# Five output buffers in layer 1's expert blocks, and layer 2's front with transposes a group ahead and additions on GpSimd

## The chip, the core and the metric

The kernel runs on one core of one Trainium2 chip, with its engines TensorE (PE in the profile; PEld is its weight load), VectorE (DVE), ScalarE (ACT), GpSimd (POOL) and SyncE (SP, here only a queue for transfers). The metric is the device time of one execution in microseconds: 1908.99 us before the change, the median of three runs (1906.96 to 1911.32). Beside these runs stands one profiled execution, from which all durations and positions come. Positions are microseconds from the start of its span.

## The reference, cut to what matters

Four layers work on x of 2708 rows and 256 columns, each with a graph part over a 2708 x 2708 adjacency matrix and then a feed-forward part:

```python
x = x + L1_gnn(layernorm(x), adj)
x = x + L1_ffn(layernorm(x))       # H = gelu(x W1); each row goes to one of 8 experts: prob * (H Wd[e] + bd[e])
x = x + L2_gnn(layernorm(x), adj)  # h = x W^T; masked attention from a_src, a_dst; elu(w @ h)
x = x + L2_ffn(layernorm(x))
```

The change lies at the end of L1_ffn and at the start of L2_gnn. For the latter, every row of h and two scores (the row's products with attn_src and attn_dst) must be there. All arithmetic is float32.

## The kernel before

x stays in SBUF as 22 tiles of 128 rows (the last has 20). A scheduling layer fixes at build time in which order each engine's instructions stand; that order need not be the order of the code, and each engine then works strictly in its own order. Tiles come from pools: a tile name has `bufs` places, and a new tile must wait until the readers of the one that had its place are done.

**Layer 1's expert blocks** (`Units`, lines 630 to 724). Rows are sorted by expert into blocks of 128. For each block GpSimd fetches 128 row names and weights (L519), then the 128 rows of H (tile `hs`, 512 KB, L659). SyncE loads the expert's weights and bias (`wb`, 1152 KB, three places, L1063); the load is left out where the place already holds that expert. TensorE turns `hs` (L670) and ScalarE copies the result to `hTs` (L671); TensorE then multiplies by `wb` into `yacc` (L719, two places). VectorE adds the bias and scales by the probability, into `ys` (L716, L720, L721), which has two places, and GpSimd scatters `ys` into the DRAM tensor `given` (L505). So block n + 2 can write its `ys` only once the scatter of block n has landed. `wb` comes free when L720 has read the bias from it. In the profile 24 blocks run; a conditional rest (L626) is not entered.

**Layer 2's front** (L1415 to L1446) goes over six groups of tiles, called g0 to g5 below: tiles 0 and 1, then four tiles each (`FOURS`). For a group it

- loads its rows of `given` into `mine` (two places, L56 and L61) on SyncE's queue, the first behind all scatters;
- adds them to x on VectorE, two tiles at a time (L1425);
- turns each tile on TensorE (L213), and ScalarE copies it to `xT4` (L214), one copy of 256 columns a tile;
- takes mean and variance (`stats`, L186, L187) and ScalarE makes 1/sqrt (L141, `var`);
- multiplies by the weights, 258 columns wide (`times`, L260), each tile into a PSUM bank of its own, `ps_acc`, of which there are five (`psum_pool(sums, 3, 5)`); transposes use three other banks, `ps_tmp`;
- scales the two score columns on ScalarE (`sc`, L1437, two places, cleared by GpSimd, L1433), turns them (L1354), copies them to one small tile (L1356) and sends them to DRAM (`row_scores`, L1357);
- reads them back broadcast to all partitions (`Rb`, L1361) and takes exp (`row_factor`, L1367);
- makes exps of the column scores (`hh`'s last column, `G`, `rowe`), and VectorE writes the scaled rows of `hh` out of `ps_acc` (L1445). Only then is that bank free.

**Layer 2's attention loop** (L1498 on) follows: VectorE makes `e` from `Rb`, `G` and the mask (L1506), and TensorE multiplies it with `hh` into five `ps_acc` banks at once (L1514).

Of the kernel before, what the change touches and what calls it, by code (L numbers as in the profile page):

```python
# [8 lines left out]
F32 = mybir.dt.float32  # L9
# [3 lines left out]
ALU = mybir.AluOpType  # L13
AX = mybir.AxisListType

P = 128
N = 2708
D = 256
DC = D // P
E = 8  # L20
NT = (N + P - 1) // P
W = 512
# [14 lines left out]
def rows(t):  # L37
    return min(P, N - t * P)
# [8 lines left out]
FOURS = [range(0, 2)] + [range(t, min(t + 4, NT)) for t in range(2, NT, 4)]  # L47
# [19 lines left out]
def adj_ffn4(ctx: ExitStack, tc: tile.TileContext, a: dict, out: bass.AP):  # L67
    nc = tc.nc
    v, s, g, te = nc.vector, nc.scalar, nc.gpsimd, nc.tensor

    const = ctx.enter_context(tc.tile_pool(name="const", reuse_waits="tile", bufs=1))
    work = ctx.enter_context(tc.tile_pool(name="work", reuse_waits="tile", bufs=3))
# [9 lines left out]
    def ps_tmp():  # L82
        if "spare" in pools:

            pools["spare"] += 1
            if pools["spare"] % 3 == 1:
                return pools["psum"].tile([P, 2, W], F32, name="num", bufs=2)[:, 0, :]
            if pools["spare"] % 3 == 2:
                return pools["psum"].tile([P, W], F32, name="den", bufs=2)
        return pools["psum"].tile([P, W], F32, tag="tmp", name="ps_tmp", bufs=pools["tmp"])  # L90
# [4 lines left out]
    ident = const.tile([P, P], F32, name="ident")  # L95
# [17 lines left out]
    x = const.tile([P, NT, D], F32, name="x")  # L113
# [26 lines left out]
    def lnexp(out, in_, func, **kw):  # L140
        i = s.activation(out, in_, func, **kw)  # L141
        tc.add_manual_dep(i.ins, pinned[-1].ins.name, mybir.DependencyInfo(
            mybir.DependencyClass.NoSync, mybir.DependencyReason.DATA), reason="table")
# [33 lines left out]
    def stats(tiles, src=None, by_log=False):  # L177


        G = len(tiles)  # L180
        mv = small.tile([P, G, 2], F32, name="mv", tag=f"mv{G}", bufs=2)
        v.memset(mv[:, G - 1, :], 1.0)
        for i, t in enumerate(tiles):
            r = rows(t)
            st = small.tile([P, 6], F32, name="st")
            v.bn_stats(st[:r], x[:r, t, :] if src is None else src[:r, i, :])  # L186
            v.bn_aggr(mv[:r, i, :], st[:r])  # L187
        var = small.tile([P, G], F32, name="var", tag=f"var{G}", bufs=2)
        if by_log:
            lnexp(var, mv[:, :, 1], AF.Ln, bias=eps)  # L190
            lnexp(var, var, AF.Exp, scale=-0.5)
            return mv, var
        v.tensor_scalar(var, mv[:, :, 1], EPS, None, op0=ALU.add)
        return mv, rsqrt(small, var, G)
# [14 lines left out]
    def turn_to(xT, xn, r, bank=None):  # L209

        p = ps_tmp() if bank is None else bank
        for c in range(DC):
            te.transpose(p[:, c * P : c * P + r], xn[:, c * P : (c + 1) * P], ident[:r, :r])  # L213
        s.copy(xT, p[:, : DC * P].rearrange("p (c t) -> p c t", c=DC)[:, :, :r])  # L214
# [297 lines left out]
    def behind(i, past):  # L512
        for p in past:
            tc.add_manual_dep(i.ins, p.name, mybir.DependencyInfo(
                mybir.DependencyClass.Sync, mybir.DependencyReason.DATA), reason="scattered rows")
# [114 lines left out]
    class Units(Blocks):  # L630
# [3 lines left out]
        def __init__(self, pool, given, weights, hidden):  # L634
            Blocks.__init__(self, pool, given, weights)
            self.hidden, self.named, self.places, self.got = hidden, [], [0, 0], None

            self.names = pool.tile([P, MOST, 2], F32, name="names")
            g.memset(self.names, 1.0)
            self.hs = [pool.tile([P, HC * P], F32, name="hs", tag="hs", bufs=3) for _ in range(3)]  # L640
            for h in self.hs:
                g.memset(h, 0.0)
            self.ik, self.ok = "taken1", "given1"

        def fetch_names(self, item):
            (_, ix, *_), b, past, src, full = item
# [54 lines left out]
        def pieces(self, pool, during=None):  # L701

            turned = [self.turn(pool, self.rows[0][1])]
            yield
            n = 0
            while self.rows:
                if len(self.rows) > 1:
                    turned.append(self.turn(pool, self.rows[1][1]))
                    yield
                w2, hT = self.ahead.pop(0), turned.pop(0)  # L710
                m, _ = self.rows.pop(0)
                self.more()
                if during is not None:
                    during(n)
                n += 1
                y = pool.tile([P, D], F32, name="ys", bufs=2)  # L716
                q = pools["psum"].tile([P, W], F32, name="yacc", bufs=2)[:, :D]
                for f in range(HC):
                    te.matmul(q, lhsT=hT[:, f, :], rhs=w2[:, f, :], start=(f == 0), stop=(f == HC - 1))  # L719
                v.tensor_tensor(y, q, w2[:, HC, :], ALU.add)  # L720
                i = v.tensor_scalar(y, y, m[:, 1:2], None, op0=ALU.mult)  # L721
                self.last = i.ins.name
                scatter(self.given, m[:, 0:1].bitcast(I32), y, self.given.shape[0] - 1, self.ok)
                yield
# [20 lines left out]
    for size, full in ((2 * P, True), (2 * P, False), (P, True), (P, False)):  # L745
        steps[size, full] = const.tile([P, NT], F32, name=f"steps{size}{full}")
        v.tensor_scalar(steps[size, full], count[:, :NT], float(size), float(size - 1) if full else 0.0,
                        op0=ALU.mult, op1=ALU.add)
# [36 lines left out]
    with ExitStack() as l0:  # L785
# [19 lines left out]
        gp = gnn.enter_context(tc.tile_pool(name="g0", reuse_waits="tile", bufs=3))  # L805
# [83 lines left out]
        for tiles in GROUPS:  # L889
            end = tiles is GROUPS[-1]  # L890
            own = [(t, (t - tiles[0]) * P, P) for t in tiles if t < FULL]
# [6 lines left out]
            for j in range(FULL):  # L898
                r = rows(j)
                ad = gp.tile([P, GMAX * P], F32, name="adrow", bufs=5)[:r, :w]  # L900
                i = nc.sync.dma_start(ad, a["adjT"][j * P : j * P + r, c0 : c0 + w])
# [19 lines left out]
                y = gp.tile([P, GMAX * P], F32, name="y", bufs=3)[:r, :w]  # L921
                wt = gp.tile([P, GMAX * P], F32, name="wt", bufs=4)[:r, :w]
                weigh(ad, y, wt, r)
                for p, pair in zip(acc, pairs):
                    for n in pair:
                        if n == len(own):
                            continue
                        _, k, q = own[n]
# [21 lines left out]
            for p, pair in zip(acc, pairs):  # L950
                if pair[0] == len(own):
                    continue
                t, m, q = own[pair[0]][0], len(pair), own[pair[-1]][2]
# [68 lines left out]
        for q, t0, t1 in ((P, 0, FULL), (LAST, FULL, NT)):  # L1022
            d = ps_tmp()
            for t in range(t0, t1):
                i = te.matmul(d[:q, t : t + 1], lhsT=cs[:, t * P : t * P + q], rhs=ones,
                              start=(t == t0), stop=(t == t1 - 1))
# [17 lines left out]
    with ExitStack() as l1:  # L1044
# [25 lines left out]
        gp = gnn.enter_context(tc.tile_pool(name="g1", reuse_waits="tile", bufs=2))  # L1070
# [279 lines left out]
    def row_scores(kept, scores, t0, n):  # L1350


        p = ps_tmp()
        te.transpose(p[:n, :P], scores, ident)  # L1354
        er = w_l1[:n, 0, :P]
        s.copy(er, p[:n, :P])  # L1356
        nc.sync.dma_start(kept.rearrange("t h c -> (t h) c")[t0 : t0 + n, :], er)  # L1357
# [6 lines left out]
    def row_factor(dst, kept, h, t0, n):  # L1364

        row_read(dst, kept, h, t0, n)
        lnexp(dst, dst, AF.Exp, scale=0.8)  # L1367
# [6 lines left out]
    with tc.tile_pool(name="t3", reuse_waits="tile", bufs=1) as t3:  # L1374
# [34 lines left out]
        with tc.tile_pool(name="g2", reuse_waits="tile", bufs=1) as gp:  # L1409
# [2 lines left out]
            rowe = gp.tile([P, NT, 1], F32, name="rowe")  # L1412
            Rb = gp.tile([P, NT * P], F32, name="Rb")
            kept = tc.dram_tile([NT, 1, P], F32, name="rows2")
            for tiles in FOURS:  # L1415
                n, t0 = len(tiles), tiles[0]
                o = gp.tile([P, 4, D], F32, name="mine", bufs=2)
                for i in load_tiles(nc, o, tiles, given[1], t0):
                    behind(i, scattered["given1"])
                for k in range(0, n, 2):  # L1420
                    for q, m in (((P, 2),) if rows(t0 + k + 1) == P else
                                 ((P, 1), (rows(t0 + k + 1), 1))):
                        i = k if q == P else k + 1
                        xs = x[:q, t0 + i : t0 + i + m, :]
                        v.tensor_tensor(xs, xs, o[:q, i : i + m, :], ALU.add)  # L1425
                xT = gp.tile([P, DC, W], F32, name="xT4", bufs=2)
                own = tiles_of(t0 * P, (n - 1) * P + rows(tiles[-1]))
                for t, k, r in own:
                    turn_to(xT[:, :, k : k + r], x[:r, t, :], r)
                rstd = stats(tiles, by_log=True)[1]  # L1430

                sc = gp.tile([P, 4, 2], F32, name="sc", bufs=2)
                g.memset(sc, 0.0)  # L1433
                ps = []
                for i, (t, k, r) in enumerate(own):
                    ps.append(times(xT, k, r, w_l2, D + 2, ps_acc()))
                    s.activation(sc[:r, i, :], ps[-1][:, D:], AF.Copy, scale=rstd[:r, i : i + 1])  # L1437
                row_scores(kept, sc[:, :n, 1], t0, n)
                row_factor(Rb[:, t0 * P : (t0 + n) * P], kept, 0, t0, n)
                lnexp(hh[:, t0 : t0 + n, D], sc[:, :n, 0], AF.Exp)  # L1440
                lnexp(G[:, t0 : t0 + n, 0], sc[:, :n, 0], AF.Exp, scale=-0.8)

                lnexp(rowe[:, t0 : t0 + n, 0], sc[:, :n, 1], AF.Exp, scale=-0.2, bias=ln8)
                for i, (p, (t, k, r)) in enumerate(zip(ps, own)):
                    v.tensor_scalar(hh[:r, t, :D], p[:, :D], rstd[:r, i : i + 1], hh[:r, t, D :],  # L1445
                                    op0=ALU.mult, op1=ALU.mult)  # L1446

            spread_out(hh[:, FULL, :])
            spread_out(G[:, FULL, :])
# [593 lines left out]
```

## Time and profile before

| what | value |
|---|---|
| runs | 1908.99 us, median of 3 |
| profiled execution | 1918.45 us; its span 1916.7 us |
| granted TensorE clock | 0.983 |
| busy: PE, PEld, DVE, ACT, POOL | 1826.6, 1326.0, 1097.8, 642.8, 344.1 us |
| layer 1's expert blocks: first to last product | 964.8 to 1084.5 us |
| last scatter issued; first load of `mine` issued | 1085.6; 1091.5 us |
| layer 2's front: first transpose to last product | 1095.1 to 1128.9 us |
| layer 2's attention loop begins | 1128.8 us |

The profiled execution took 9.5 us more than the median. "Busy" of TensorE includes the pipelined end of each matmul, so that a stage can be almost all busy and still have room. In the trace one fp32 product of a tile with a 128-row half of the weights is two matmul records, and a transpose is one; a tile's product with all 256 rows is thus four records.

### The profile page before, as it was taken

How to read it: one execution, taken by the hardware profiler on the slowest of the kernel's cores; microseconds unless marked ns; L12 is line 12 of the kernel's file. 1: busy time of each engine (PE TensorE's matmuls, PEld its weight loads, DVE VectorE, ACT ScalarE, POOL GpSimd, SP SyncE). 2: the span in 40 equal slices, each digit the busy share in tenths (PEclk: the TensorE clock that was granted, in tenths of full speed). 3: DMA queues.
4: the chain of work that ended last, by engine and by line, in shares of the span. 5: the costliest groups of instructions: out<-in, count | busy, mean ns of one | idle time of the engine just before them, and what ended most of it. 6: DMA issues, size and time to landing. Idle time of an engine off the chain costs nothing.

```text
span 1916.7 us, 25790 instructions
## 1 busy us (share of the span) xinstructions
PE 1826.6 (95%) x9453; PEld 1326.0 (69%) x9453; DVE 1097.8 (57%) x2498; ACT 642.8 (34%) x1459; POOL 344.1 (18%) x406
## 2 busy tenths in 40 slices
PE   7999998999999999999979799999899999999998
PEld 6888777888888888888778578888566632232344
DVE  6777862443433625354532265555355398999897
ACT  7868751222222303113222232222232551031131
POOL 1004254333322001303356300000000000000000
PEclk9999999999998999999989899999899999999999
DMA  8435656887773554544758410000101000000000
GB/s 276 139 109 161 219 187 223 318 331 279 279 284 107 178 150 121 142 105 136 211 161 319 141 50 1 1 1 1 44 1 34 17 1 23 23 12 28 20 20 16
DMA packets 88846, 233.33 MB, mean 122 GB/s; under 512 B 18015, under 2 KB 44679, under 8 KB 80648
## 3 DMA queue, kind: packets, MB, share of 16 engines
q1 hardware_dynamic: 71752, 189.18, 29.9%
q0 software_dynamic: 16960, 42.42, 7.0%
q8 instruction: 78, 1.28, 0.3%
q14 instruction: 56, 0.46, 0.1%
HBM read 216.29 MB, written 28.71 MB: 128 GB/s over the span
## 4 chain that ended last, share of the span: by engine, by line
PE 42%; DVE 2%; DMA 2%; ACT 2%; issue 1%; another core or an unknown queue 1%; POOL 0%; SPq 0%; POOLq 0%; DVEq 0%; ACTq 0%
PE num L1941 10%; PE ps_acc L1514 9%; PE den L1951 6%; PE ps_tmp L367 4%; PE ps_acc L1704 3%; PE yacc L719 3%; PE ps_tmp L260 2%; DMA L_ffn_beta<-in_L_ffn_beta 1%; PE ps_acc L670 1%; PE ps_acc L260 1%; PE ps_tmp L213 1%; DVE e L1911 1%; DVE e L1506 0%; ACT wh L1843 0%
## 5 line engine op out<-in xcount | busy, mean ns | idle before, releaser
L1911 DVE SCALAR_TENSOR_TENSOR e<-arena,G,mask 128x1024 f32<-128x1024 f32 (+1 forms) x264 | 287.0, 1149 | 13.6 <-PE den L1951 13.6
L1941 PE MATMUL num<-e,wh 128*64 128x512 f32 (+4 forms) x1056 | 215.8, 551 | 0.0
L1514 PE MATMUL ps_acc<-hh,e 128*128 128x257 f32 x882 | 199.2, 382 | 1.7 <-ACT o L1457 1.7
L1300 PE MATMUL acc<-sup,adrow 128*128 128x256 f32 x882 | 200.1, 384 | 0.4 <-DVE adrow L1268 0.4
L929 PE MATMUL acc<-msg,wt 128*128 128x256 f32 x882 | 198.6, 381 | 2.0 <-DVE wt L887 1.2
L1300 PEld LDWEIGHTS acc<-sup,adrow 128*128 128x128 f32 x882 | 166.0, 191 | 29.1 <-issue 5.6
L929 PEld LDWEIGHTS acc<-msg,wt 128*128 128x128 f32 x882 | 165.2, 190 | 28.4 <-issue 2.1
L1514 PEld LDWEIGHTS ps_acc<-hh,e 128*128 128x128 f32 x882 | 163.6, 190 | 29.2 <-ACT o L1457 4.3
L617 PE MATMUL yacc<-wb,hTs 128*128 128x256 f32 x736 | 170.6, 383 | 6.2 <-issue 3.4
L583 PE MATMUL ps_acc<-xTs,wa 128*128 128x256 f32 (+1 forms) x768 | 169.3, 373 | 5.8 <-DVE xTs L573 3.1
L585 ACT ACTIVATE hTs<-ps_acc,wa 128x256 f32<-128x256 f32 (+1 forms) x192 | 88.8, 465 | 247.1 <-PE yacc L617 164.5
L583 PEld LDWEIGHTS ps_acc<-xTs,wa 128*128 128x128 f32 x768 | 136.5, 190 | 32.1 <-DVE xTs L573 5.6
L617 PEld LDWEIGHTS yacc<-wb,hTs 128*128 128x128 f32 x736 | 138.3, 192 | 25.3 <-issue 3.8
L1941 PEld LDWEIGHTS num<-e,wh 128*64 128x64 f32 (+1 forms) x1056 | 66.5, 136 | 127.3 <-issue 105.6
L1506 DVE SCALAR_TENSOR_TENSOR e<-Rb,G,mask 128x640 f32<-128x640 f32 (+2 forms) x110 | 85.1, 774 | 90.5 <-PE ps_acc L1514 90.4
L1951 PE MATMUL den<-e,wh 128*32 128x512 f32 (+4 forms) x1056 | 118.0, 548 | 0.0
L214 ACT COPY xT<-ps_tmp 128x256 f32<-128x256 f32 x98 | 33.6, 365 | 235.9 <-PE ps_tmp L213 218.3
L1265 DVE TENSOR_SCALAR mask<-adrow 128x1024 uint8<-128x1024 f32 (+1 forms) x66 | 41.4, 627 | 123.2 <-DMA adrow<-in_adjT 122.8
L719 PE MATMUL yacc<-wb,hTs 128*128 128x256 f32 x384 | 88.7, 385 | 1.1 <-DMA wb<-in_L_ffn_Wdp 1.1
L887 DVE SCALAR_TENSOR_TENSOR wt<-adrow,wt 128x640 f32<-128x640 f32 (+3 forms) x67 | 71.1, 1063 | 27.5 <-ACT wt L141 19.8
L1951 PEld LDWEIGHTS den<-e,wh 128*32 128x32 f32 (+1 forms) x1056 | 30.2, 108 | 77.9 <-issue 73.8
L619 DVE TENSOR_TENSOR ys<-yacc,wb 128x256 f32<-128x256 f32 x46 | 19.5, 424 | 112.7 <-PE yacc L617 103.4
(457 smaller groups left out, 2618.7 us busy)
## 6 DMA issues: line engine op xcount, KB each, us to landing
adhalf<-in_adjT SPq DMA_DIRECT2D x42, 677.0 KB
wb<-in_L_ffn_W2p SPq DMA_DIRECT2D x24, 1152.0 KB
wb<-in_L_ffn_Wdp SPq DMA_DIRECT2D x24, 1152.0 KB
wa<-in_L_ffn_W1b SPq DMA_DIRECT2D x24, 1028.0 KB
adrow<-in_adjT SPq DMA_DIRECT2D x42, 512.0 KB
adrow<-in_adjT SPq DMA_DIRECT2D x42, 320.0 KB
adrow<-in_adjT SPq DMA_DIRECT2D x21, 576.0 KB
adrow<-in_adjT SPq DMA_DIRECT2D x21, 448.0 KB
```

What stands on the lines that cost most here:

```text
L367: te.matmul(p[:, :w], lhsT=w1[:, c, f * P : (f + 1) * P], rhs=xnT[:, c, c0 : c0 + w], start=(c == 0), stop=(c == DC - 1))
L583: i = te.matmul(p[:, f % 2, : m * P], lhsT=w1[:, c, f * P : (f + 1) * P], rhs=xT[:, c, : m * P], start=(c == 0), stop=(c == DC - 1))
L585: s.activation(hT[:, f, : m * P], p[:, f % 2, : m * P], AF.Gelu, bias=bias[:, f : f + 1])
L617: te.matmul(q[:, k, :], lhsT=hT[:, f, k * P : (k + 1) * P], rhs=w2[:, f, :], start=(f == 0), stop=(f == HC - 1))
L719: te.matmul(q, lhsT=hT[:, f, :], rhs=w2[:, f, :], start=(f == 0), stop=(f == HC - 1))
L929: te.matmul(p[:q, n - pair[0], :], lhsT=wt[:, k : k + q], rhs=msg[:r, j, :], start=(j == 0 and n == pair[0]), stop=(j == FULL - 1 and n == ...
L1300: te.matmul(p[:q, n - pair[0], :], lhsT=ad[:, k : k + q], rhs=sup[:, jj, :], start=(jj == 0 and n == pair[0]), stop=(jj == FULL - 1 and n ...
L1506: i = v.scalar_tensor_tensor(e[:r, :w], Rb[:r, c0 : c0 + w], G[:r, j, :], mask[:r, j, c0 : c0 + w], op0=ALU.max, op1=ALU.mult)
L1514: te.matmul(p[:, : D + 1], lhsT=e[:, k : k + q], rhs=hh[:, j, :], start=(j == 0), stop=False)
L1911: v.scalar_tensor_tensor(e[:, :w], slow[:, m % 2, k, :w], G[:, j, 2 * pair + k, :], mask[:, j, c0 : c0 + w], op0=ALU.max, op1=ALU.mult)
L1941: te.matmul(num[k * DK : (k + 1) * DK, hf, :q], lhsT=wh[some, j, 2 * pair + k, :DK], rhs=e[some, h0 - c0 : h0 - c0 + q], start=(j == 0), s ...
L1951: te.matmul(den[z : z + Q, :q], lhsT=wh[some, i, 2 * pair + k, DK : DK + 1] .to_broadcast([some.stop - some.start, Q]), rhs=e[some, h0 - c ...
```

## The change

Layer 1: the block counter `outputs` gives three of every five blocks a `y` from another pool, the tile `xn` of `work`, which has three places; two of five keep `ys`. There are so five places in turn.

Layer 2's front is split into two functions. `turned_up` loads a group, adds, turns and copies, and takes the statistics. `valued` multiplies, makes the exps and writes `hh`. A group is turned up before the group ahead of it is multiplied. The additions of g2 to g5 (those from `FOURS[2]` on) are on GpSimd. Transposes of two tiles share one bank, and one ScalarE copy of 512 columns takes both. `row_scores` of a group comes after the transposes of the next one or two, and `row_factor` after that; the rows of `hh` are written ahead of `G` and `rowe` in the code.

```diff
-            self.ik, self.ok = "taken1", "given1"
+            self.ik, self.ok, self.outputs = "taken1", "given1", 0
...
-                y = pool.tile([P, D], F32, name="ys", bufs=2)
+                self.outputs += 1
+                y = (pool.tile([P, D], F32, name="ys", bufs=2) if self.outputs % 5 < 2 else
+                     work.tile([P, D], F32, name="xn"))
...
-            for tiles in FOURS:
+            def turned_up(tiles):
                 n, t0 = len(tiles), tiles[0]
+                adder = v if t0 < FOURS[2][0] else g
                 o = gp.tile([P, 4, D], F32, name="mine", bufs=2)
                 for i in load_tiles(nc, o, tiles, given[1], t0):
                     behind(i, scattered["given1"])
+                xT = gp.tile([P, DC, W], F32, name="xT4", bufs=2)
                 for k in range(0, n, 2):
...
-                        v.tensor_tensor(xs, xs, o[:q, i : i + m, :], ALU.add)
-                xT = gp.tile([P, DC, W], F32, name="xT4", bufs=2)
-                for t, k, r in own:
-                    turn_to(xT[:, :, k : k + r], x[:r, t, :], r)
-                rstd = stats(tiles, by_log=True)[1]
+                        adder.tensor_tensor(xs, xs, o[:q, i : i + m, :], ALU.add)
+                    p = ps_tmp()
+                    for i in range(2):
+                        q = rows(t0 + k + i)
+                        for c in range(DC):
+                            te.transpose(p[:, (c * 2 + i) * P : (c * 2 + i) * P + q],
+                                         x[:q, t0 + k + i, c * P : (c + 1) * P], ident[:q, :q])
+                    s.copy(xT[:, :, k * P : (k + 1) * P + r],
+                           p.rearrange("p (c t) -> p c t", c=DC)[:, :, : P + r])
+                return tiles, xT, stats(tiles, by_log=True)[1]
+
+            def valued(tiles, xT, rstd):
...
                 for i, (t, k, r) in enumerate(own):
                     ps.append(times(xT, k, r, w_l2, D + 2, ps_acc()))
                     s.activation(sc[:r, i, :], ps[-1][:, D:], AF.Copy, scale=rstd[:r, i : i + 1])
-                row_scores(kept, sc[:, :n, 1], t0, n)
-                row_factor(Rb[:, t0 * P : (t0 + n) * P], kept, 0, t0, n)
                 lnexp(hh[:, t0 : t0 + n, D], sc[:, :n, 0], AF.Exp)
...
+            ahead, todo = [turned_up(FOURS[0])], list(FOURS[1:])
+            for k in range(len(FOURS)):
+                sc, t0, n = valued(*ahead.pop(0))
+                while todo and len(ahead) < 2:
+                    ahead.append(turned_up(todo.pop(0)))
+                    if len(ahead) == 1:
+                        row_scores(kept, sc[:, :n, 1], t0, n)
+                if k > 0:
+                    row_scores(kept, sc[:, :n, 1], t0, n)
+                row_factor(Rb[:, t0 * P : (t0 + n) * P], kept, 0, t0, n)
```

The order in which the changed instructions stand, as built: TensorE has the eight transposes of g2 among the products of g1, and those of g3, g4 and g5 between the products of g1 and g2, g2 and g3, g3 and g4. GpSimd has the nine additions in a row, with one clearing of `sc` between those of g3 and g4. VectorE has the statistics of g3, of g4 and of the first half of g5 ahead of the four writes of `hh` of g1; three of the first four `e` stand ahead of the writes of `hh` of g3, where before it were two. On SyncE's queue the rest of g5's `mine` moves ahead of the first `Rb`; the first send of scores stands, as before, between the loads of g4 and g5. In layer 1 no instruction moves; only the tile and the waits of VectorE's L720 change.

## The prediction

> **What bounds the kernel now.** I read the page's first part, then the waits of each engine where the diff works, then the chain of waits. The page's busy times:
>
> ```profile
> PE 1826.6 (95%) x9453; PEld 1326.0 (69%) x9453; DVE 1097.8 (57%) x2498; ACT 642.8 (34%) x1459; POOL 344.1 (18%) x406
> ```
>
> TensorE is the bound over the whole, so an edit pays only where it closes a gap or a wait of TensorE. VectorE and GpSimd have room.
>
> Layer 1, the timeline of VectorE and TensorE (start, duration, engine, line, tiles; idle before and its releaser in brackets):
>
> ```profile
> 1073.02 3.69 PE L719 MATMUL yacc<-wb,hTs 128*128 128x256 f32 x16 [1.10 <-DMA wb<-in_L_ffn_Wdp]
> 1074.53 0.42 DVE L720 TENSOR_TENSOR ys<-yacc,wb 128x256 f32<-128x256 f32 x1 [6.96 <-DMA given<-ys,names]
> ```
>
> The second line is what five buffers attack: L720 ready, but its place in `ys` still being scattered. It was about 3.5 us late there, 0.75 at 1077.47 and 0.2 to 1.2 at some other blocks. Yet TensorE hardly saw it: between 1003 and 1056 its products and transposes follow one another without a gap, 4.33 us a block. Its one wait of size is the first line, 1.10 us for weights; that load was issued at 1062.9, when an L720 that was on time had freed its place. One larger gap stands apart:
>
> ```profile
> 992.40 1.07 ACT L671 COPY hTs<-ps_acc 128x512 f32<-128x512 f32 x2 [11.01 <-remote]
> 993.04 1.97 PE L670 MATMUL ps_acc<-ident,hs 128*128 128x128 f32 x8 [8.75 <-ACT hTs L671]
> ```
>
> No engine and no transfer works in those 8.75 us, and the releaser is none of the kernel's. I take it, with a smaller one of about 1 us near 1055, as peculiar to this execution: together they are the 9.5 us by which it exceeds the median. Neither number goes into a gain.
>
> The front, in the chain of waits (start, us, what), around g4:
>
> ```profile
> 1113.94 3.50 PE ps_acc L260 x16
> ...
> 1117.63 0.62 ACT Rb L141
> 1118.25 0.19 ACT L_gnn_W L1356
> 1118.44 0.11 ACT hh L141
> 1118.55 0.09 ACT G L141
> 1118.64 0.19 ACT rowe L141
> 1118.83 0.26 ACT xT L214
> 1119.09 0.04 issue
> 1119.13 0.44 PE ps_tmp L213 x2
> 1119.57 3.50 PE ps_acc L260 x16
> ```
>
> After a group's last product ScalarE has a queue of small things, and the last `xT` copy of the next group stands behind them, so the products start 2.13 us after the ones before ended. The starts of g2 to g5 are 1107.23, 1113.94, 1119.57, 1125.06: 5.56 to 6.7 us a group, against 3.50 of products, 0.88 of transposes and 0.1 of scores, 4.48.
>
> **What the Trainium skill says.** "GPSIMD Engine Reference", section 3.1, prices an fp32 addition of 2048 elements on GpSimd at 4497 ns, VectorE at 2293. The trace has GpSimd only at 256 columns, 718 ns (L1833), and VectorE at 512, 671 ns. "SBUF — State Buffer", section "Who interferes with whom": a VectorE instruction with two SBUF inputs contends with a GpSimd instruction that reads SBUF, one with a single input does not. The statistics and `hh` (PSUM) have one; `e` has more. No overlap of this kind is in the trace. "TensorE: Matmul & The Clock Gate", part 1: after idling, TensorE starts at half clock for about 3.4 us. The trace agrees: g0's product records take 0.477 us, later ones 0.219. "Perfetto Trace Analysis", section "Optimizing Scalar/DVE Operations", says each instruction carries an overhead and grouping helps; in the trace two copies of 256 columns cost 2 x 0.365, one of 512 0.586.
>
> **The change, part by part.** All against the profiled execution.
>
> *Five buffers.* The lateness of L720 goes, and with it nothing on TensorE that I can see; an earlier L720 can free `wb` earlier (its load waits for it). In this execution that is 0; I take 0.4, bounds 0 and 3. The three places shared with `xn` have no other user in this stage. The scatter keeps its order, and the end (last product 1084.49, scatter issued 1085.62, landed about 1090.7, `mine` 1091.51) is one chain without a buffer wait: 0.
>
> *GpSimd's additions.* An addition of 128x512, d: the straight line through 718 ns at 256 and the page's 4497 at 2048 gives 1.26 (estimate); the page scaled alone 1.12; twice 718, without shared overhead, 1.44. I take 1.3; g2's two wait for the load landed at 1098.3 and then end 1098.35 + 2d = 1100.95, g3's 1103.55. The load of g4 needs g2's place: issued 1101.0 (before 1100.3), landed at 1104.1 with the 3 us that such a load takes, added by 1106.7; g5's first by 1107.9. On VectorE ten additions leave; their 0.67 each costs nothing there.
>
> *Front, group by group* (products end before; after):
>
> - g0 1100.08; 1100.87. Its one copy stands behind an exp on ScalarE, later by 0.8. Cold clock as before.
> - g1 1105.57; 1106.9. Its transposes follow at once, to 1101.8. ScalarE makes `sc`, three exps (0.75) and two copies of 0.59; products start at 1102.5, and the eight transposes of g2 (0.88) stand among them: 1102.5 + 3.50 + 0.88. That time was paid here, not lost.
> - g2 1110.88; 1111.95. With transposes of g3 the second product could go at 1108.8. But five `ps_acc` banks are all held, and g1's must be emptied by `hh`, ahead of which VectorE now has the statistics of g3, g4 and half of g5. These wait for GpSimd's additions: the first of g5 ends 1107.9, two statistics with their aggregates take 0.9 and `hh` 0.54, so the bank is free about 1109.3. Wait about 0.5.
> - g3 1117.44; 1116.45. 0.88 of transposes, 0.11 of scores, 3.50; nothing late.
> - g4 1123.07; 1121.5. Here the readback bites: g0's `Rb` exp waits on ScalarE to about 1108.7, g1's scores go out after it (sends took 1.2 to 2.7, readbacks about 3.3 us), its `Rb` lands about 1115.1, and three `e` of 0.86 stand ahead of `hh` of g3 on VectorE, to 1118.3. The second product of g4 starts 1118.9 instead of 1118.3: wait 0.6.
> - g5 1128.85; 1125.4 (0.30 shorter transposes already done; 3.79 and 0.1).
>
> So the end of the last product moves by 1128.85 - 1125.4 = 3.45; bounds 2.2 (both waits doubled) and 4.6 (none). The ideal, five groups of 5.56 down to 4.48, would be 5.4; 0.8 is lost at g0, the rest to the two waits.
>
> *Behind.* L1514 starts right at g5's last product in before and is bound by TensorE from there; the last `hh` keeps its offset, so the shift passes to the end. Earlier `e` are no gain.
>
> Sum: 0.4 + 3.45 = 3.9; profiled 1918.45 to 1914.6 if the odd stall recurred, median 1908.99 to about 1905.0.
>
> **Rivals.**
>
> *Buffers bring more.* In runs without the odd stall the blocks stand closer in time, transfers crowd more, and late L720 may turn into late `wb` loads. For: the wait of 1.10 for weights, and L720 3.5 us late beside it; SyncE's queue did wait for L720. Against: that load was not delayed by it. Up to 3 us in place of 0.4: about 1902.
>
> *The front gives little.* The waits at g2 and g4 are sums of several round trips that I worked out by hand; if readbacks take 2 us more, or VectorE reaches `hh` of g1 2 us later, each wait grows by that much. For: no slack of over 0.6 us at either. Against: sends and readbacks have durations in the trace. Gain 1.5: about 1907.5; no difference to be told.
>
> *Slower: GpSimd's addition.* Place: `hh` of g1 behind g5's first addition on VectorE's queue. Seven additions lie ahead of that statistic: 1098.35 + 7d + 0.9 + 0.54 = 1099.8 + 7d is when g2's second product can go (below d = 1.4 the loads decide, as above). From 1109.3 on every later microsecond is lost: the gain of 3.85 is gone at d = 1.9, and the kernel is 3.8 us slower at d = 2.45, 4 at 2.5, which it could reach if a two-input GpSimd instruction and VectorE's `e` and g1's additions lock each other, or the 512-column form is handled worse than 256. About 1913. Against: 718 ns at 256 and 1.12 from the page; little with two SBUF inputs runs on VectorE between 1098 and 1108.
>
> That the change does nothing is possible for the buffers alone, covered by 0; in the front the order of TensorE's instructions as built does change.
>
> **How the numbers follow.** 0.2% is 3.8 us, about what a measurement of this kernel can tell from no change; the forecast lies on that border. Forecast 0.55, its own range 1903 to 1907 (front 2.2 to 4.6, buffers 0 to 1.3), a little over half of it beyond the border: 0.30 faster, 0.25 same. Buffers more: 0.20, all faster. Front little: 0.17, same. Slower: 0.08. Sums: faster 0.50, same 0.42, slower 0.08. The range, 1900 to 1911, takes in the first three with the full 3 and 4.6 us and about 1.5 us of spread between runs (1906.96 to 1911.32 before), and most of the small losses; what is left out is a real loss and a gain beyond 9.
>
> **What would show it.** In the profile after: additions of 128x512 (L1431) on GpSimd at 1.1 to 1.45 us each (2 and more: the slower rival). L720 with no idle time ended by the scatter `given<-ys,names`, and TensorE's time from first to last product of the blocks (without the odd stall) within 1 us of before: buffers right; 2 or 3 us shorter: the first rival. Front from first transpose to last product 33.8 us before, 30.3 after; a wait of about 0.5 us before g2's second product, released by VectorE's `hh`, and one before g4's, with `e` ahead of `hh` of g3. The starts of the products of g3 to g5 4.5 to 5.1 us apart. If g1's `hh` comes after 1110.5, or g0's `Rb` exp holds ScalarE long enough to hold a copy of `xT4`, the working failed there. Wrong altogether would be a changed period of the blocks, or a loop behind the front that waits for something new, for instance `Rb` of the last group, since its send now comes later in the code.

## The result and the profile after

| | before | changed |
|---|---|---|
| median of 22 runs | 1908.82 us | 1905.03 us |
| lowest, highest | 1905.56, 1915.64 | 1896.22, 1910.66 |
| ratio, 95% interval | | 0.9974 (0.9965 to 0.9984) |
| profiled execution's span | 1916.7 us | 1900.2 us |
| stage of layer 1's blocks, first to last product | 119.7 us | 118.5 us |
| layer 2's front: first load of `mine` to the loop's first product | 37.27 us | 35.13 us |
| from there to the end | 787.9 us | 788.9 us |

The two spans differ by 16.5 us, and the table shows that the stages of the change hold only 3.3 of it. Put one trace beside the other, the changed execution is 13 to 14 us ahead when the blocks of layer 1 begin; 11.5 us of that arise around the blocks of layer 0 (positions 256 to 315), which the diff doesn't touch. From its 1201st to its 1501st matmul record TensorE needs 71.8 us before, 71.5 to 74.6 us in the profiles of all twelve experiments below, and 60.3 us in this one profile of the changed kernel alone. So the spans of two profiles can't be subtracted; stages can.

The front is read from the first load of `mine` (1091.51 before, 1076.23 after), called M below. The page's busy times of the changed kernel, and its timeline of VectorE and TensorE in layer 1:

```profile
PE 1821.4 (96%) x9453; PEld 1325.5 (70%) x9453; DVE 1094.9 (58%) x2489; ACT 642.2 (34%) x1448; POOL 352.3 (19%) x415
```

```profile
995.36 1.94 PE L670 MATMUL ps_acc<-ident,hs 128*128 128x128 f32 x8 [7.37 <-DMA hs<-hid,names]
...
1061.67 0.42 DVE L722 TENSOR_TENSOR xn<-yacc,wb 128x256 f32<-128x256 f32 x1 [3.52 <-PE yacc L721]
1066.00 0.42 DVE L722 TENSOR_TENSOR xn<-yacc,wb 128x256 f32<-128x256 f32 x1 [3.52 <-PE yacc L721]
```

No idle time of L722 (L720 before) is ended by a scatter any more, where before there were six such waits with 23.4 us; in the lines shown it waits for its product. TensorE's blocks are nonetheless 4.33 us apart, as before. And TensorE has a large gap again, 7.37 us, here ended by a gather of rows.

The front's chain of waits, from g2's load to g2's second product (start, us, what):

```profile
1079.77 3.72 DMA mine<-given
1083.49 0.07 issue
1083.57 2.50 POOL x L1431 x2
1086.07 0.02 issue
1086.09 4.16 DMA mine<-given
1090.25 0.07 issue
1090.32 3.74 POOL x L1431 x3
1094.07 0.02 issue
1094.09 0.04 DVE st L186
...
1094.43 0.41 DVE st L186
1094.84 0.46 DVE hh L1454
1095.30 0.04 issue
1095.34 2.88 PE ps_acc L260 x12
```

GpSimd adds g2, which frees its place; g4's load takes 4.16 us; GpSimd adds g4 and the first half of g5; VectorE takes their statistics and writes the first `hh` of g1; only then has TensorE a bank. The timeline of TensorE has the same place as a wait, and the groups by shape give the price of an addition:

```profile
1092.93 1.04 PE L260 MATMUL ps_acc<-w_l,xT 128*128 128x258 f32 x4
1095.34 2.88 PE L260 MATMUL ps_acc<-w_l,xT 128*128 128x258 f32 x12 [1.38 <-DVE hh L1454]
```

```profile
L1431 POOL TENSOR_TENSOR x<-x,mine 128x512 f32<-128x512 f32 x7 | 8.7, 1272 | 9.4 <-DMA mine<-given 9.4
L1438 ACT COPY xT<-ps_tmp 128x512 f32<-128x512 f32 x10 | 5.6, 576 | 0.1
```

After that wait TensorE starts g3 and g4 one after the other, 4.6 us apart, without another wait for `hh`.

### The profile page after: what moved, and what is told of

Its sections match the earlier page's. It is cut to its first block, busy times and chain, and to the rows that moved or that the text cites. A ratio compares the mean times of both kernels' runs of the same rounds, so it can differ in the third digit from the quotient of the medians.

```text
span 1900.2 us, 25781 instructions
## 1 busy us (share of the span) xinstructions
PE 1821.4 (96%) x9453; PEld 1325.5 (70%) x9453; DVE 1094.9 (58%) x2489; ACT 642.2 (34%) x1448; POOL 352.3 (19%) x415
## 4 chain that ended last, share of the span: by engine, by line
PE 39%; DVE 4%; DMA 4%; issue 1%; ACT 1%; POOL 1%; POOLq 0%; SPq 0%; DVEq 0%; ACTq 0%
PE num L1965 10%; PE ps_acc L1538 9%; PE den L1975 5%; PE ps_tmp L367 4%; PE ps_acc L1728 3%; PE yacc L721 2%; PE ps_tmp L260 2%; DVE e L1935 1%; DMA names<-taken,b_ix 1%; DMA L_ffn_beta<-in_L_ffn_beta 1%; PE ps_acc L260 1%; PE ps_acc L670 1%; DMA mine<-given 1%; PE ps_tmp L213 0%; DMA hs<-hid,names 0%
## 5 line engine op out<-in xcount | busy, mean ns | idle before, releaser
L931 PEld LDWEIGHTS acc<-msg,wt 128*128 128x128 f32 x882 | 165.8, 191 | 27.5 <-DVE wt L889 1.8
L1267 DVE TENSOR_SCALAR mask<-adrow 128x1024 uint8<-128x1024 f32 (+1 forms) x66 | 41.2, 625 | 122.6 <-DMA adrow<-in_adjT 122.2
L214 ACT COPY xT<-ps_tmp 128x256 f32<-128x256 f32 x76 | 26.8, 367 | 219.9 <-PE ps_tmp L213 219.7
L505 POOL DMA_INDIRECT given<-ys,xs x46 | 65.3, 1420 | 79.3 <-DVE ys L620 66.1
```

What stands on the lines that cost most here:

```text
L931: te.matmul(p[:q, n - pair[0], :], lhsT=wt[:, k : k + q], rhs=msg[:r, j, :], start=(j == 0 and n == pair[0]), stop=(j == FULL - 1 and n == ...
```

## Experiments

Two theories at the start. **A**: the front gave the 2.1 us of its profile (2.2 in the texts below), the five places the rest of the 3.8 us between the medians. **B**: the places gave nothing, and what the front leaves of the 3.8 us is scatter between runs. Then: what holds the front back. Two figures of each run are used: the ratio to the kernel before, timed beside it, and the profile's own length from M to the attention loop's first product, called the front. The front repeated to 0.4 us in the changed kernel (35.13, 35.04 and 34.77) and to 0.8 us in the old one (37.27, 37.08 and, in e8, 36.47), so a smaller difference between two single profiles says little.

### Buffers alone (e1)

```diff
-                y = pool.tile([P, D], F32, name="ys", bufs=2)
+                self.outputs += 1
+                y = (pool.tile([P, D], F32, name="ys", bufs=2) if self.outputs % 5 < 2 else
+                     work.tile([P, D], F32, name="xn"))
```

> The five output places alone, layer 2's front as before. In the two profiles the front accounts for 2.2 us (last product 37.34 us after the first load of mine before, 35.14 after), while the medians differ by 3.8. Theory A, the buffers gave the other 1.6 or more by the places of wb that come free earlier: ratio 0.9990 to 0.9980, and no L720 whose idle time is ended by the scatter. Theory B, they gave 0.4 or less, as predicted, and the rest is scatter between runs: ratio 0.9998 to 1.0002. The front by the profile: 37.3 us from the first load of mine to the last product, as before, under both.

Ratio 1.0011 (1.0001 to 1.0021); blocks 120.6 us, front 37.1. No L722 waits for a scatter, and nothing is gained: the interval leaves out A's 0.9990. It lies just above 1, for which the profile shows no cause. The timeline of TensorE also answers another point:

```profile
995.81 1.97 PE L670 MATMUL ps_acc<-ident,hs 128*128 128x128 f32 x8 [8.72 <-ACT hTs L671]
```

The gap that the prediction took as peculiar to one execution is here again: it begins 19.5 us after the stage's first product, as in the profile before.

### Front alone (e2), and the change once more (e5)

```diff
-                self.outputs += 1
-                y = (pool.tile([P, D], F32, name="ys", bufs=2) if self.outputs % 5 < 2 else
-                     work.tile([P, D], F32, name="xn"))
+                y = pool.tile([P, D], F32, name="ys", bufs=2)
```

> The new front alone, two places of ys in layer 1. By its profile the front must read as in the changed kernel: wait of TensorE for hh ahead of g2's second product 1.4 us, last product 35.1 us after the first load of mine. Theory A: ratio about 0.9988 (2.2 us), less than the whole change has. Theory B: the whole gain is here, 0.9980 or lower.

e5 is the changed kernel without an edit.

> The changed kernel itself, beside the same runs of the kernel before as the other three of this call. The two parts alone measured 1.0011 (buffers) and 0.9993 (front), the whole 0.9974, in another call. Theory B (the front alone gives 2.2 us, the buffers nothing): ratio 0.9988, interval within 0.9975 to 1.0000, and the stage of blocks as long as in the other profiles, 117 to 121 us. Theory A (the buffers help once the new front follows): 0.9978 or lower again.

The front alone: 0.9993 (0.9982 to 1.0005), 34.8 us by the profile. The whole change: 0.9996 (0.9980 to 1.0011), 35.0 us, blocks 117.2 us. Both intervals hold 0.9989, what 2.1 us would be; neither holds the 0.9974 of the first comparison. As it was put before e2, B wanted the whole gain from the front, 0.9980 or lower, and e2 leaves that out. That e5 gave no more than e2 speaks for B as it stands above: the rest of the first comparison's gain came with neither part alone, nor again with both. The kernel before itself took 1908.8 us there and 1919 to 1921 us in all later comparisons, so that the interval of one comparison may not cover what differs from one to another.

Why the first comparison was better than either by some 4 us (0.0019 and 0.0022) is open. One candidate is on record: the stretch around layer 0's blocks, which took 60.3 us in one execution and 71.5 us or more in the thirteen others. If a part of the first comparison's executions went through it as fast as that one, medians there would move by up to 11 us, in either kernel. That is not shown, since of each set of runs only one execution has a profile.

### One place instead of two (e8)

The suspected wait, made large, in the kernel before.

```diff
-                y = pool.tile([P, D], F32, name="ys", bufs=2)
+                y = pool.tile([P, D], F32, name="ys", bufs=1)
```

> The kernel before with one place of ys in place of two: the wait that five places take away is made as large as can be. A block then needs L720, L721, the scatter's issue 1.1 us after L720 and its landing some 5 us later before the next L720, 6 to 6.5 us in place of 4.33. If the wait for the scatter reaches TensorE as soon as it outlasts the two places of yacc: the stage of 24 blocks takes 145 to 156 us in place of 119.7, ratio 1.013 to 1.019. If the gathers on GpSimd hold the blocks anyway: within 5 us of before.

Ratio 1.0173 (1.0142 to 1.0203, two runs), blocks 145.9 us. The waits in the stage (engine, line, what it waited for: us, times, longest), of VectorE with two places and with one, then of TensorE with one:

```profile
DVE ys L720 <- DMA given<-ys,names: 23.4, 6, 7.0
```

```profile
DVE ys L720 <- DMA given<-ys,names: 76.3, 14, 8.8
```

```profile
PE yacc L719 <- DVE ys L720: 16.4, 6, 5.0
```

With one place the wait reaches TensorE. With two, VectorE waited 23.4 us in all and TensorE not once for L720: the wait was short enough for the two places of `yacc` to take it up. So five have nothing to give.

### Three places for mine (e3)

```diff
-                o = gp.tile([P, 4, D], F32, name="mine", bufs=2)
+                o = gp.tile([P, 4, D], F32, name="mine", bufs=3)
```

> The changed kernel with three places for mine instead of two, so that g4's load waits for no addition and GpSimd's additions run on without a gap. If g2's wait (1.38 us) comes from the late load of g4 (landed 3.8 us after issue, 1.5 us of idle GpSimd ahead of g4's additions), hh of g1 comes 1.3 to 1.9 us earlier, the wait falls below 0.3, and the last product stands at 33.7 to 34.2 us from the first load instead of 35.1: ratio about 0.0006 below that of the changed kernel. If GpSimd's additions themselves hold it (seven of 1.27 us), it stays within 0.3 us of 35.1.

Front 33.3 us, a little better than expected; TensorE has no wait for `hh` any more, and GpSimd goes from g3's additions to g4's (the second line) without a gap:

```profile
1105.26 4.96 POOL L1431 TENSOR_TENSOR x<-x,mine 128x512 f32<-128x512 f32 x4 [7.01 <-DMA mine<-given]
...
1110.21 5.09 POOL L1431 TENSOR_TENSOR x<-x,mine 128x512 f32<-128x512 f32 x5
```

So the 1.4 us came through the load that waits for a place. Ratio 0.9989 (0.9976 to 1.0002).

### The same with g0's tiles copied apart (e4)

```diff
+                    if t0 == FOURS[0][0]:
+                        for i in range(2):
+                            turn_to(xT[:, :, (k + i) * P : (k + i + 1) * P], x[:, t0 + k + i, :], P)
+                        continue
                     p = ps_tmp()
```

> As e3, and g0's two tiles are turned one by one with a copy of 256 columns each, as before the change, which also takes g1's first transpose away from ahead of g0's products. Before, g0's products began 4.75 us after the first load of mine, in the changed kernel 5.96. If the single copy behind the exp and that transpose cost these 1.2 us, they begin at 4.7 to 4.9 here; but if g2's second product is still held by hh of g1, this gain is swallowed there, and the last product stands as in e3. If not swallowed: 1.2 us earlier than e3, near 32.8.

g0's products begin 4.69 us after M, as before the change; front 32.9 us, only 0.3 better than e3, which two single profiles can't tell from no difference; ratio 0.9989 (0.9977 to 1.0000). g1's products begin at 10.75, 0.8 earlier than in e3: half of the 1.6 us by which g0's begin earlier than in e3 is swallowed between g0 and g1, and more ahead of g2's second product, which comes only 0.4 earlier.

### All additions on VectorE (e6)

```diff
-                adder = v if t0 < FOURS[2][0] else g
+                adder = v
```

> The changed kernel with all additions of the front back on VectorE, looking ahead as before. An addition is 0.67 us in place of 1.27 and starts 0.05 us after its load landed in place of 0.46; mine's places come free earlier, so g4's load too. If GpSimd's chain of loads and additions is what holds hh of g1, g2's second product starts at about 17.0 us from the first load of mine in place of 19.1, and the last product ends at 33.0 to 33.8 in place of 35.1. If VectorE becomes the bound instead (7 additions, 4.7 us, more on it), it is 35 or later.

Front 32.7 us, ratio 0.9982 (0.9971 to 0.9993). The timeline of TensorE, products of g1 to g4:

```profile
1097.11 3.22 PE L260 MATMUL ps_acc<-w_l,xT 128*128 128x258 f32 x14
1101.14 3.65 PE L260 MATMUL ps_acc<-w_l,xT 128*128 128x258 f32 x16
1105.62 3.65 PE L260 MATMUL ps_acc<-w_l,xT 128*128 128x258 f32 x16
1110.19 4.09 PE L260 MATMUL ps_acc<-w_l,xT 128*128 128x258 f32 x18
```

No bracket, so no wait: from g2 on the groups follow 4.5 to 4.6 us apart. VectorE, 27.5 us busy of 32.7, has the room. The new front with its additions left on VectorE takes 32.7 us, the old one 36.5 to 37.3; moving the additions to GpSimd gives some 2.3 us of that back. How much of the gain is the look-ahead's and how much the shared copies' was not separated.

### GpSimd's additions doubled (e7)

```diff
                         adder.tensor_tensor(xs, xs, o[:q, i : i + m, :], ALU.add)
+                        if adder is g:
+                            g.tensor_tensor(o[:q, i : i + m, :], o[:q, i : i + m, :], o[:q, i : i + m, :], ALU.add)
```

> The changed kernel with a second GpSimd addition of equal size after each of those of g2 to g5 (mine to itself, its sum is read by nothing). By the chain (four instructions for each of g2 and g3 and g4, one for g5 ahead of the statistic) hh of g1 comes 5.9 us later: g2's second product at 25.0 us from the first load of mine, the last product at 40.8 to 41.0, the whole 5.7 us slower than the changed kernel, ratio about 1.002 to before. If TensorE has room behind g2 to take this back, the last product ends before 39.

Front 41.2 us, ratio 1.0026 (1.0006 to 1.0046): the forecast of the end held, but not by its steps. g2's second product came at 23.35 us, not 25.0, because the added instruction, which reads the same operand twice, was cheaper than one with two:

```profile
L1431 POOL TENSOR_TENSOR x<-x,mine 128x512 f32<-128x512 f32 x7 | 8.7, 1262 | 8.1 <-DMA mine<-given 8.1
...
L1433 POOL TENSOR_TENSOR mine<-mine 128x512 f32<-128x512 f32 x7 | 7.1, 1030 | 0.0
```

Six of 0.23 us are 1.4 of the 1.65 us. The end caught up with the forecast because TensorE, after 5.5 us of waiting, took 4.72 us in place of 2.88 for the twelve records behind it, most of that time at a granted clock of 0.50:

```profile
1112.48 4.72 PE L260 MATMUL ps_acc<-w_l,xT 128*128 128x258 f32 x12 [5.51 <-DVE hh L1456]
```

### GpSimd's additions without the look-ahead (e10)

```diff
-                        v.tensor_tensor(xs, xs, o[:q, i : i + m, :], ALU.add)
+                        (v if t0 < FOURS[2][0] else g).tensor_tensor(xs, xs, o[:q, i : i + m, :], ALU.add)
```

> The kernel before with nothing changed but the additions of g2 to g5 on GpSimd, no group turned up ahead. The build puts the statistics of g3, g4 and half of g5 ahead of hh of g1 here too. If that is what makes the wait, the last product ends 2 to 3 us later than before, 39 to 40 us after the first load of mine in place of 37.3, with TensorE waiting for hh of g1 ahead of g2's second product. If the additions are hidden without the look-ahead: 37.0 to 37.5.

38.3 us in its one execution: 1.0 to 1.8 later than in the three profiles of the old front, less than expected. The wait is at g2's second product, but the profile names ScalarE as its end:

```profile
1111.57 2.88 PE L260 MATMUL ps_acc<-w_l,xT 128*128 128x258 f32 x12 [1.53 <-ACT xT L214]
```

The first `hh` of g1 ended at 1111.3, the copy at about 1111.5. That copy stood on ScalarE behind the exp of g0's `Rb`, which had waited 2.17 us for its readback. Both were late together, so taking one away here would have changed little.

### Every tile copied apart (e11)

```diff
-                    p = ps_tmp()
...
-                    s.copy(xT[:, :, k * P : (k + 1) * P + r],
-                           p.rearrange("p (c t) -> p c t", c=DC)[:, :, : P + r])
+                    for i in range(2):
+                        q = rows(t0 + k + i)
+                        turn_to(xT[:, :, (k + i) * P : (k + i) * P + q], x[:q, t0 + k + i, :], q)
```

> The changed kernel with every tile turned into a bank of its own and copied alone (256 columns), so that only the shared copy is undone. ScalarE then has 4 x 0.365 in place of 2 x 0.586 a group, 0.29 more. If the shared copy is worth something: last product up to 0.5 us later than the 35.1 of the changed kernel. If the wait for hh of g1 sets the end, it stays at 34.8 to 35.2, though g0's products begin at 4.7 in place of 5.6 to 6.0.

37.1 us, 2 us later than the changed kernel, which neither case foresaw. The windows view has the reason for most of it (window, length, busy time and number of instructions of each engine, granted clock, DMA share, GB/s):

```profile
1108.60:1112.20 3.60, 1.79 (x9) 1.09 (x8) 3.08 (x11) 1.51 (x6) 2.92 (x5) 1.00 0.03 10
1112.20:1115.60 3.40, 3.40 (x10) 2.65 (x9) 1.70 (x9) 0.91 (x4) 0.00 (x0) 0.50 0.32 77
```

Two waits, 0.86 us for the copy (behind the same exp of `Rb`) and 0.95 for `hh`, fell into one stretch in which TensorE was busy half of the time; the next 3.4 us ran at half clock, and cost 1.7 us. "TensorE: Matmul & The Clock Gate" of the Trainium skill, part 1, describes a clock that is set by windows of about 3.4 us of activity; the length agrees, the granted clock stood at half for 3.41 us here. In the changed kernel the 1.38 us wait brought no such drop. g2's second product itself began 18.9 us after M, no later than in the changed kernel (19.1), so without the drop the end would have come near 35.4 us (an estimate, 37.1 less 1.7). What the shared copy is worth this run can't say: it is one profile, and whether the drop comes in each execution wasn't tried.

### Put together (e9), and without the five places (e12)

e9 is the edits of e6 and of e4's g0; e12 is e9 with the two places of `ys` again (the edit of e2).

> The changed kernel with all additions on VectorE and g0's two tiles turned and copied one by one, put together from e4 and e6. In e6 nothing held g2's products, so the earlier start of g0's (4.7 us after the first load of mine in place of 5.4) should now reach the end: last product at 31.9 to 32.2 us in place of 32.71, ratio to the kernel before 0.9972 to 0.9982. If ScalarE or VectorE hold g1's products anyway, it stays at 32.6 to 32.8.

> The kernel of e9 with two places of ys in layer 1 again, so without the five. e9 measured 0.9968 (0.9957 to 0.9978) with a front 5.1 us shorter by the profile (0.27%, so 0.9973 from the front alone). Theory B, the five places give nothing: the interval overlaps that of e9, and the stage of blocks is 117 to 121 us in the profile. Theory A, they give 1.6 us or more: ratio 0.9976 or higher. The front as in e9: last product 32.1 to 32.3 us after the first load of mine.

e9: 0.9968 (0.9957 to 0.9978), front 32.2 us. e12: 0.9974 (0.9965 to 0.9983), front 32.3 us, blocks 118.2 us. The intervals overlap widely, so nothing is seen of the five places here either; but e12's also holds the 0.9976 of theory A, so these two runs alone don't decide, and e1 and e8 weigh more. e9's lies wholly below that of e5, the changed kernel in the later comparisons, but overlaps that of the first one; the front is shorter than the changed kernel's by 2.6 to 3.0 us in the profiles. Nothing on record speaks for keeping the five places.

Over all profiles, the stage of blocks took 119.7, 117.3, 119.7 and 118.2 us with two places (mean 118.7) and 116.2 to 120.6 with five (nine profiles, mean 118.4). The 0.3 us between the means is far within the spread.

## Why the prediction was right, and where it was not

The time, 1905.0, was met by the median, 1905.03, and the ratio's interval lies on the faster side. The mechanism was right: the front gains, by transposes that stand ahead of the products, and a bank that waits for `hh` of g1 behind GpSimd's additions takes part of it back. But the agreement to the tenth is luck: by the profile the front gave 2.1 us, not 3.45, just under the low bound set for it, the places gave nothing in place of 0.4, and the other 1.7 us are in neither stage of the change. The second comparison of the same kernel measured 0.04%, with an interval that ends at 0.2%.

**Five buffers, 0.4 with bounds 0 and 3.** What the runs show is nothing, by e1, e8, e12 and the lengths of the stage. The reading that L720's lateness hardly reached TensorE was right; the rival that buffers bring more is not supported.

**The odd stall.** Wrong: "peculiar to this execution" fell, and with it the reading that no engine and no transfer works there. TensorE, VectorE and ScalarE stand still, but in those 8.75 us GpSimd is busy for 5.0 us issuing gathers and scatters, and transfers move 0.67 MB. A gap of TensorE begins 19.5 us after the stage's first product in 13 of the 14 profiles, with two places and with five; it lasts 5.7 us with one place (e8) and 7.9 to 10.2 us in the others. The changed kernel's first profile has none there, but one of 7.37 us later in the stage. So a gap of this kind is part of the stage in every profile, and was not the 9.5 us by which one execution exceeded the median. What causes it is open.

**GpSimd's price, 1.3 us.** Measured 1.27. The slower rival needed 1.9 and more; the straight line between the trace's 718 ns and the 4497 ns of the Trainium skill ("GPSIMD Engine Reference", section 3.1) gave 1.26, an estimate.

**g0, 0.8 late.** Right in kind, and nearly in size: from M, g0's products ended 1.05 us later in the first profile and 0.66 in e5. But one of g1's transposes stands ahead of g0's products and waits for VectorE's addition, which the working did not see.

**g2's wait, 0.5.** Measured 1.38, 1.73 (e5) and 1.29 (e2): the step that failed. Not GpSimd but the loads were mis-sized. From issue to GpSimd's start the three loads took 3.80, 3.80 and 4.23 us (1079.77 to 1083.57, 1082.49 to 1086.29, 1086.09 to 1090.32), where the working had some 3.1 and a start at once, and g4's was issued 0.4 later. The sum makes the first addition of g5 end 1.4 us late, and `hh` with it. e3 shows it: with a third place the wait is gone.

**g4's wait, 0.6, behind three `e`.** Did not come. The three `e` did stand ahead of `hh` of g3, to 1103.67, but TensorE was itself 1.5 us later by then, so the bank, free at 1104.1, was asked for only about 1104.5.

**The end.** The shift passed on, except for about 1 us between loop and end (787.9 before, 788.9 after); since e1, with the old front, has 789.1, that is not the change's.

**Slips of the working that changed nothing.** Nine additions leave VectorE, not ten (2498 instructions before, 2489 after). The four starts that it lists are 5.49 to 6.71 us apart, and from the end of g0's products to the end of g5's the five groups took 28.8 us, 5.76 each, so the ideal gain was 6.4 us and not 5.4. Both waits doubled would have left 2.35, not 2.2. The two odd gaps, 8.75 and 1.37 us, are 10.1 together, not 9.5.

## What to carry to other kernels

Look ahead on the engine that is the bound, and then ask which wait ends last: here a PSUM bank, held by a small write on VectorE, behind statistics that wait for another engine. Moving work to an idle engine helps only if the engine that it leaves was the late one: VectorE had room, and GpSimd at twice the time, in a chain of load, addition and free place, gave back about half of the gain. And a wait that shows 23 us on an engine off the bound can be worth nothing: make it larger and see when it reaches the bound.

## What was not expected of the hardware

- A GpSimd addition that reads one operand twice took 1.03 us at 128x512, with two operands 1.26 (e7).
- A wait of 5.5 us (e7), or two of some 0.9 within 3 us (e11), was followed by products at half clock, for 3.8 us and 3.4 us: 1.8 and 1.7 us lost beside the waits. Each is one execution.
- One stretch of the program that no edit touches took 60.3 us in one execution and 71.5 to 74.6 us in thirteen others.
- Two comparisons of one kernel with the same kernel before gave 0.9974 (0.9965 to 0.9984) and 0.9996 (0.9980 to 1.0011), while the kernel before itself moved by 10 us, 0.5%. An effect of 0.1% is better read from the stage in the profile, and from more than one profile.
